# Moving maxima and logit transposes to VectorE, rounding copies to GpSimd, and the first side loads to a later unit, in a planned attention and mixture-of-experts layer

## The chip, the cores and the metric

The kernel runs on one core of a Trainium2 chip. The metric is device time in microseconds of that core; three runs of the kernel before gave a median of 3115.78 us (3114.96 to 3122.53). A difference of about 0.3% is what measurement can tell from none.

## The reference

One transformer layer in float32 over x of 4 batches, 2048 tokens, 256 channels. First attention with 16 heads of 16 channels, then a feed-forward part with a shared expert and 8 routed experts (top 2 of 8, chosen within 2 of 4 groups):

```python
x = x + attn(layernorm(x))        # 16 heads of 16; softmax(q k / 16) v; w_o, b_o, and its own + x
xf = layernorm(x).reshape(-1, 256)
scores = softmax(xf @ w_gate.T)   # 8 experts; biased, grouped top 2
shared = silu(xf @ sw1.T) * (xf @ sw3.T) @ sw2.T
out = shared.at[flat_idx].add(routed_out)   # the routed rows are added by the number in flat_idx
x = x + out
```

`flat_idx` holds expert numbers 0 to 7, so the routed results of all tokens end in the first 8 rows.

## The kernel before, in words

**Units.** Attention is cut into 64 units: one batch, one group of four heads, one chunk of 512 queries. A unit walks over 16 key tiles of 128 keys. Three kinds of TensorE (PE) work belong to it:

- `mx` (64 matmuls): scores with queries on the partitions, one PSUM bank each; VectorE (DVE) reduces each 128x512 bank to a row maximum `ms`. They run some 22 key tiles ahead of the rest.
- `st` (64 matmuls): scores with keys on the partitions, in which row 63 of the stacked queries `qst` carries the negative maximum; ScalarE (ACT) turns each bank into `et` by an exponential.
- `av` (16 groups of four matmuls, eight in the trace): the weighted sum of values, with a column of ones for the denominator.

`mx` and `st` use half of the PE's rows each (63 or 64 of 128), so two of them, one in each half, run side by side. Seven PSUM banks serve all matmuls but `av`, and a bank is reused when its reader (DVE or ACT) is done.

**From the maxima to the queries.** When a unit's last `ms` is there, `finish_mx` reduces it to `mm` (128x16) on DVE, queues a PE transpose of it to `mt` (the queue `urgent`), ACT copies it with sign changed to `mr` (16x128), and two DMAs of 4 KB write it into rows 63 and 127 of `qst`. Until then no `st` of that unit may be issued (`turned`).

**Side work.** Between the attention matmuls stand pieces of the other work, as generators that yield what they need next: `qkv_first` (load a chunk of x of a later batch, write the pad rows of its stacked keys and queries in DRAM, `kd` and `qd`), `norm`, `qkv` (transposes to channels `pt_x`, projections `pp` and `pv`), `post` (output projection `po`, second norm, transposes, shared expert `pa`, `pb`, `pd`), `route` (logits `lgT`, then their transpose `lg`), `setup` (loads and splits the weights of `post`).

**High and low parts.** float32 products are made of three matmuls on rounded numbers (fp32r): a high part h is the rounded value, a low part l the rest. In `to_channels`, `qk_proj`, `halves` and `shared` ACT writes h, in the first two straight from the PSUM bank (`S.copy(h, pt)`, or `hi` from `pp`) beside the full value (`f`, two buffers named `qkf`), and GpSimd (POOL) makes l from f and h. POOL cannot read PSUM.

**What sets the order.** A planner at build time (`Plan`, `Ahead`) gives PE, DVE and POOL a fixed order: it searches orders of `mx`, `st`, `av` and side pieces with costs written in the code. A piece tells what it costs ACT: 940 ns by default. ACT's order is fixed too, as issued. The DMA queue of SyncE (SP) is in order, and at most eight of its DMAs are under way: each waits for the one eight places before it.

**At the start.** Before unit 0 a hand-written prologue makes queries and keys of batch 0. Then `rest` makes the projections of head groups 2 and 3, the chunk loads of batch 1 start as soon as their gate is open, and `setup` is queued when unit 1 begins (`enter`). `load_unit` loads the `qst` (512 KB) of a later unit and, when the head group changes, 2 MB of keys `kst`.

All engine instructions stand under line L55 in the profile, that of a recording helper, so that one goes by tile names. A name such as `mt<-cs,mm` means tile `mt` written from `cs` (constants) and `mm`.

Of the kernel before, what the change touches and what calls it, by code (L numbers as in the profile page):

```python
# [20 lines left out]
P = 128  # L21
# [15 lines left out]
LATE = 0.01, 0.1, 16  # L37
TURNS = 1600
NET = 6
BANKS = 7  # L40
# [330 lines left out]
def const_array(rows):  # L371

    cols, at, parts = {}, 0, []

    def put(name, a):
        nonlocal at
        a = np.broadcast_to(np.asarray(a, np.float32), (P, np.shape(a)[-1]))
        cols[name] = (at, at + a.shape[1])
        parts.append(a)
        at += a.shape[1]  # L380

    i = np.arange(P)
    put("ident", np.eye(P))
    put("ones", np.ones((P, P)))
    e = np.arange(E)
    put("tri8", (e[None, :] < e[:, None]).astype(np.float32).reshape(1, -1))
    g = np.arange(4)
    put("tri4", (g[None, :] < g[:, None]).astype(np.float32).reshape(1, -1))
    put("below", (i[:, None] < np.arange(E + 1)[None, :]).astype(np.float32))
    put("pair", (i[:, None] % 64 == np.arange(64)[None, :]).astype(np.float32))  # L390
    put("eight", (i[:, None] % 32 == np.arange(8)[None, :]).astype(np.float32))
    nt = rows // P
    put("rows", (2 * (np.arange(nt)[None, :, None] * P + i[:, None, None]) + np.arange(2)[None, None, :]).reshape(P, -1))
    return np.ascontiguousarray(np.concatenate(parts, 1)), cols
# [9 lines left out]
def body(tc, B, L, cols, x, wqkv, bqk, wst, bst, bv, wo, bo, wg, w1, w2, w3, sw1, sw2, sw3, ebias, cst, pad, out):  # L404
# [20 lines left out]

    def need(kind, ns=0, *tiles, more=0):


        return kind, ns, tiles, more

    def gate(open_):

        return "g", open_, (), 0

# [122 lines left out]
    def to_channels(src, name, keep=None, fast=False, out=None):  # L557

        h, l = out or hl(f"t_{name}")
        if not fast:  # L560
            for c in range(2):
                f = keep[:, c, :] if keep is not None else sb.tile([P, QC], F32, tag="qkf", name=f"f_{name}{c}", bufs=2)
                pt = stile(f"pt_{name}{c}")
                for i in range(TQ):
                    T.transpose(pt[:, i * P:(i + 1) * P], src[:, i, c * P:(c + 1) * P], ident)
                S.copy(f, pt)
                S.copy(h[:, c, :], pt)
                G.tensor_tensor(l[:, c, :], f, h[:, c, :].bitcast(F32), ALU.subtract)
                if c == 0:
                    yield need("s1", 436)  # L570
            return h, l
        for c in range(2):
            pt = mtile(f"pt_{name}{c}")
            for i in range(TQ):
                T.transpose(pt[:, i * P:(i + 1) * P], src[:, i, c * P:(c + 1) * P], ident)
            S.copy(keep[:, c, :], pt)
            S.copy(h[:, c, :], pt)
            V.tensor_tensor(l[:, c, :], pt, h[:, c, :].bitcast(F32), ALU.subtract)
            yield
        return h, l  # L580
# [8 lines left out]
    def qk_proj(b, c, m, alloc=None):  # L589
# [15 lines left out]
        S.activation(f, pp, AF.Identity, bias=b_qk[:, m:m + 1])  # L605
        if alloc:
            S.copy(hi, f)
        else:
            S.activation(hi, pp, AF.Identity, bias=b_qk[:, m:m + 1])
        mark["G"] = G.tensor_tensor(lo, f, hi.bitcast(F32), ALU.subtract).ins  # L610
# [49 lines left out]
    def qkv_first(b, c):  # L660

        yield gate(lambda: prev(b, c, 2) in stored)
        load_x(b * NPER + c)
        tok = slice(c * QC, (c + 1) * QC)
        fill_rows(kd[b], 0, 0, H, tok)
        fill_rows(qd[b], 16, 0, H, tok)
        yield gate(lambda: prev(b, c) in stored and prev(b, c) in turned_x)
        yield need("d", 420, xin[b * NPER + c], more=3)
        yield from norm(b, c)
        normed.add((b, c))  # L670
        sums.append(store(b, c))
# [6 lines left out]
    def qkv(b, c):  # L678

        yield gate(lambda: (b, c) in normed)  # L680
        yield need("s1", 436, xls[b, c], more=1)
        xTs[b, c] = yield from to_channels(xls[b, c], f"x{b}_{c}", out=hl(f"t_x{b}_{c}", "hq"))
        turned_x.add((b, c))
        for k, m in enumerate((2, 3, 0, 1)):
            yield need("s2", 705, *xTs[b, c], more=5 - k)
            yield from qk_proj(b, c, m)
        for half in range(2):
            yield need("s2", 705, *xTs[b, c], more=1 - half)
            yield from v_proj(b, c, half)
        del xTs[b, c]  # L690
# [6 lines left out]
    def route(ch, x2T):  # L697
        n = f"{ch}"
        r = lambda nm, shape, dt=F32: sb.tile(shape, dt, tag="r_" + nm, name=f"{nm}_{n}", bufs=1)
        yield need("s1", 300, x2T)  # L700
        lgT = stile(f"lgT_{n}")
# [4 lines left out]
        f4_dead.add(f"x2T_{RN[ch]}")  # L706
        lgs = r("lgs", [P, P])
        S.copy(lgs, lgT[:, 0:P])
        yield need("m1", 109, lgs)
        lg = mtile(f"lg_{n}")  # L710
        T.transpose(lg[:, 0:P], lgs, ident)
        l3 = lg[:, 0:P].rearrange("p (t e) -> p t e", e=32)[:, :, 0:E]
        b3 = lambda a, w=E: a.unsqueeze(2).broadcast_to([P, TQ, w])
# [241 lines left out]
    def halves(b, c, ahl):  # L955

        yield gate(lambda: (b, c) in scaled)
        aT, parts = scaled.pop((b, c))
        yield need("a", 1060, aT)
        for t, np_ in parts:  # L960
            S.copy(ahl[0][0:np_, t, :], aT[0:np_, t, :])
            G.tensor_tensor(ahl[1][0:np_, t, :], aT[0:np_, t, :], ahl[0][0:np_, t, :].bitcast(F32), ALU.subtract)
        f4_dead.add(f"aT_{b}_{c}")

    def post_a(b, c, ahl=None, space=None):
# [22 lines left out]
        yield gate(lambda: f4_free(1))  # L988
        yield need("s1", 436, x2, more=1)
        x2T = f4(f"x2T_{n}")  # L990
# [37 lines left out]
    def shared(ch, n, x1, x2T, x2hl):  # L1028
# [5 lines left out]
        for m in range(2):  # L1034
# [14 lines left out]
            if m == 0:  # L1049
                yield need("s2", 705, more=1)  # L1050
        yield need("a", 920, hT)
        hhl = hl(f"hT_{n}")
        S.copy(r2(hhl[0]), r2(hT))
        G.tensor_tensor(r2(hhl[1]), r2(hT), r2(hhl[0]).bitcast(F32), ALU.subtract)
# [136 lines left out]

    urgent = deque()
    turned = set()
    qz = []

# [21 lines left out]
    def finish_mx(u, ms):  # L1217
        mm = sb.tile([P, 4 * TQ], F32, tag="mm", name=f"mm_{u}", bufs=2)
        V.tensor_reduce(mm, ms.rearrange("p h q k -> p (h q) k"), AX.X, ALU.max)

        def tr(alloc=stile):
            pt = alloc(f"mt_{u}")
            ins = T.transpose(pt[0:4 * TQ, 0:P], mm, ident).ins
            mr = sb.tile([4 * TQ, P], F32R, tag="mr", name=f"mr_{u}", bufs=2)
            S.activation(mr, pt[0:4 * TQ, 0:P], AF.Copy, scale=-1.0)
            for j in range(2):
                r0 = 64 * j + 63
                Q.dma_start(
                    qst[u % 3][r0:r0 + 1].bitcast(F32).rearrange("o p (a n) -> o (p a) n", n=P),
                    mr[2 * TQ * j:2 * TQ * j + 2 * TQ, :].bitcast(F32))  # L1230
            turned.add(u)
            return ins

        urgent.append((need("s1", 109, mm), tr))

# [120 lines left out]
    with tc.manual_schedule(engines={ENG.PE, ENG.DVE, ENG.Pool}):  # L1356
# [42 lines left out]
        load_v(0)  # L1399
        urgent.popleft()[1](mtile)  # L1400
        p30, p32 = qp(3, 0), qp(3, 2)
# [12 lines left out]
    def rest():  # L1414
        for c, m in [(c, m) for m in (1, 3) for c in range(4)]:
            yield need("s2", 705, *xTs[0, c], more=3 - c)
            yield from qk_proj(0, c, m)
        for c in range(4):
            del xTs[0, c]
# [33 lines left out]
    def enter(u):  # L1453

        b, g, c = units[u]
        if u == 1:
            posts.append(setup())
# [65 lines left out]
    def heads():  # L1523

        for n, fn in list(urgent)[:1]:
            yield n, (lambda fn=fn: (urgent.popleft(), fn()))
        for jobs in (side, sums, norms, firsts) + ((queue, posts) if due() > 0.5 * rate() else (posts, queue)):
# [3 lines left out]
    def light():  # L1531

        t, soon = plan.clock["PE"], INF
        for n, go in heads():
            kind, cost, tiles, _ = n
            if kind == "g":
# [35 lines left out]

    def urgent_now():
        while urgent:
            urgent.popleft()[1]()

    def give(c):
# [4 lines left out]
        elif c == "S":  # L1582
            u = ns // (4 * NK)
            while u not in turned:
                if nm < (u + 1) * NK * MXS:
                    do_m()
                else:
                    urgent_now()
            do_s()
# [12 lines left out]
    def present():  # L1602
# [10 lines left out]
        for n, go in heads():  # L1613
            if n[0][0] in "ms":
                ns_ = n[1] + (705 if n[0][1] == "2" else 0)
                blocks += (1 + n[3]) * [(plan.when(*n[2]) + 55, ns_, 598 if n[0][0] == "m" else 0, 160 if ns_ < 200 else 940)]
            elif n[0] == "d":
# [80 lines left out]
    with tc.manual_schedule(engines={ENG.PE, ENG.DVE, ENG.Pool}):  # L1698
        while na < NS:
# [24 lines left out]
            if plan.clock["PE"] == before:  # L1724

                urgent_now()
                plan.clock["PE"] += 500
        while urgent:
            urgent.popleft()[1]()
    ordered.__exit__(None, None, None)  # L1730
# [68 lines left out]
```

## Time and profile before

| | us |
|---|---|
| median of three runs | 3115.78 |
| the profiled execution | 3116.26 |
| its span, first to last instruction | 3114.5 |
| first exponential of unit 0 begins at about | 98 |
| PE busy, share of the span | 3022.1, 97% |
| DVE busy | 2806.9, 90% |
| ACT busy | 2510.0, 81% |
| POOL busy | 549.0, 18% |
| mean granted PE clock | 0.984 |

The page and the views are of one execution. Busy time of the PE is that of matmuls under way, with modelled ends, so a PE that is 97% busy need not be at its peak. A row of a group names engine, operation, tiles, shape and count, then busy time and mean duration, then the idle time of that engine just before and what ended it. "PEld" are weight loads, which belong to the PE's queue but overlap its matmuls.

### The profile page before, as it was taken

What the parts mean: (1) busy time and instruction counts of PE and PEld (TensorE: products, weight loads), DVE (VectorE), ACT (ScalarE), POOL (GpSimd) and SP (SyncE); (2) the same over time, 40 slices, a digit from 0 to 9 for tenths busy, and PEclk for the clock granted to TensorE, in tenths of its full rate; (3) what the DMA queues carried; (4) which work ended last, traced back from release to release, by engine and by line L of the source; (5) the groups of instructions that cost most, each with busy time, mean ns of one, the idle gap of its engine ahead of it and who ended that gap; (6) DMA issues with size and microseconds to landing.
All of it is one profiled execution on the core that took longest, in us unless ns stands there. A gap on an engine that the chain in (4) does not pass through costs nothing.

```text
span 3114.5 us, 52652 instructions
## 1 busy us (share of the span) xinstructions
PE 3022.1 (97%) x19507; PEld 1372.0 (44%) x19507; DVE 2806.9 (90%) x5049; ACT 2510.0 (81%) x4982; POOL 549.0 (18%) x503
## 2 busy tenths in 40 slices
PE   7799999999999999999999999999999999999987
PEld 5334444444444444444444444444444444444436
DVE  7689999998999999999999999899999999999926
ACT  5488888887888888888888888878887887887774
POOL 5222112211211021102211111110121111012213
PEclk9899999999999999999999999999999999999998
DMA  5644544232121212022121211212120201011200
GB/s 153 213 149 114 153 124 131 74 106 99 62 78 46 86 32 91 25 81 94 63 71 56 75 40 50 98 38 92 43 75 28 78 25 67 30 53 39 76 25 15
DMA packets 142236, 237.32 MB, mean 76 GB/s; under 512 B 13531, under 2 KB 71003, under 8 KB 137819
## 3 DMA queue, kind: packets, MB, share of 16 engines
q1 hardware_dynamic: 141979, 233.96, 23.7%
q8 instruction: 153, 2.51, 0.3%
q14 instruction: 104, 0.85, 0.1%
HBM read 138.38 MB, written 111.80 MB: 80 GB/s over the span
## 4 chain that ended last, share of the span: by engine, by line
PE 79%; DVE 14%; DMA 3%; ACT 2%; issue 1%; POOL 1%; SPq 0%; ACTq 0%; POOLq 0%; DVEq 0%
PE av L55 28%; PE mx L55 19%; PE st L55 19%; DVE ms L55 11%; PE pp L55 3%; PE po L55 2%; PE pd L55 1%; PE pv L55 1%; PE pb L55 1%; DMA qd<-hi 1%; ACT et L55 1%; PE pa L55 1%; PE pt_x L55 1%; PE mu L55 1%; PE pg L55 1%
## 5 line engine op out<-in xcount | busy, mean ns | idle before, releaser
L55 DVE TENSOR_REDUCE ms<-mx 128x1 f32<-128x512 f32 x4096 | 2533.1, 681 | 200.9 <-PE mx L55 134.2
L55 ACT ACTIVATE et<-st 128x512 f32<-128x512 f32 x4096 | 2138.1, 614 | 395.4 <-PE st L55 282.7
L55 PE MATMUL mx<-kst,qst 63*128 63x512 f32 x3984 | 1227.5, 444 | 22.9 <-DMA qst<-qd 9.9
L55 PE MATMUL st<-qst,kst 64*128 64x512 f32 x4032 | 1217.2, 443 | 25.5 <-ACT et L55 7.3
L55 PE MATMUL av<-et,vst 128*32 128x512 f32 x8192 | 1100.3, 608 | 0.0
L55 PEld LDWEIGHTS st<-qst,kst 64*128 64x128 f32 x4032 | 570.6, 186 | 604.3 <-DVE ms L55 282.4
L55 PEld LDWEIGHTS mx<-kst,qst 63*128 63x128 f32 x3984 | 575.5, 186 | 575.2 <-DVE ms L55 256.1
L55 PEld LDWEIGHTS av<-et,vst 128*32 128x32 f32 x8192 | 164.5, 108 | 326.6 <-issue 305.6
L55 POOL TENSOR_TENSOR lo<-qkf,hi 128x512 fp32r<-128x512 f32 x64 | 82.1, 1283 | 377.0 <-ACT hi L55 330.6
L55 POOL TENSOR_TENSOR th<-th,cs 128x512 f32<-128x512 f32 x32 | 33.4, 1044 | 374.6 <-ACT th L55 374.6
L55 POOL TENSOR_TENSOR aT<-aT,rb 128x512 f32<-128x512 f32 (+1 forms) x32 | 40.8, 1281 | 297.5 <-DMA rb<-rd 297.2
L55 POOL TENSOR_TENSOR hT<-hT,th 128x512 f32<-128x512 f32 x32 | 41.1, 1283 | 230.5 <-ACT hT L55 107.7
L55 ACT ACTIVATE qkf<-pp,b_qk 128x512 f32<-128x512 f32 x64 | 44.1, 689 | 45.3 <-PE pp L55 45.1
L55 POOL TENSOR_TENSOR rs_b<-rs_b,nhalf 128x4 f32<-128x4 f32 x16 | 16.3, 1017 | 230.9 <-DVE rs_b L55 185.7
L55 POOL TENSOR_TENSOR x<-x,xl 128x256 f32<-128x256 f32 x64 | 46.4, 754 | 10.6 <-ACT xl L55 10.4
L55 POOL TENSOR_TENSOR x<-x,b_o 128x256 f32<-128x256 f32 x64 | 45.3, 742 | 0.0
L55 ACT ACTIVATE hi<-pp,b_qk 128x512 fp32r<-128x512 f32 x56 | 38.3, 683 | 4.5 <-DMA qd<-hi 4.5
L55 ACT COPY ao<-av 128x512 f32<-128x512 f32 x63 | 37.9, 601 | 4.1 <-PE av L55 3.6
L55 ACT ACTIVATE xl<-x,rs_a 128x256 f32<-128x256 f32 x64 | 33.4, 595 | 9.3 <-DVE rs_a L55 9.3
L55 ACT ACTIVATE x<-x,rs_b 128x256 f32<-128x256 f32 x64 | 33.4, 597 | 7.7 <-DVE rs_b L55 7.7
L55 POOL TENSOR_TENSOR th<-th,sg 128x512 f32<-128x512 f32 x30 | 38.7, 1291 | 2.4
L55 ACT ACTIVATE hT<-pb 128x512 f32<-128x512 f32 x32 | 19.2, 600 | 22.7 <-PE pb L55 15.0
(400 smaller groups left out, 2200.1 us busy)
## 6 DMA issues: line engine op xcount, KB each, us to landing
kst<-kd SPq DMA_DIRECT2D x16, 2048.0 KB
qst<-qd SPq DMA_DIRECT2D x63, 512.0 KB
qd<-hi SPq DMA_DIRECT2D x64, 256.0 KB
kd<-hi SPq DMA_DIRECT2D x64, 256.0 KB
ad<-ao SPq DMA_DIRECT2D x63, 256.0 KB
vst<-vd SPq DMA_DIRECT2D x19, 664.0 KB
vd<-vt SPq DMA_DIRECT2D x32, 332.0 KB
x<-x SPq DMA_DIRECT2D x16, 512.0 KB
```

The costliest lines, as they stand in the source:

```text
L55: r = f(*a, **k)
```

## The change

Five edits go together.

1. **Maxima.** `finish_mx` folds the sign into the reduction, turns the 128x32 tile `mm` on DVE in blocks of 32x32 to `mt`, and four DMAs with pieces of 128 bytes write it to `qst`. The PE transpose, ACT's copy and the queue `urgent` go.
2. **Logits.** `route` turns the 128x128 logits on DVE, from PSUM to SBUF; ACT's copy `lgs`, the PE transpose `lg` and its bank go. The blocks put another order of tokens on the partitions, and the constant `rows` follows it.
3. **High parts.** In the slow form of `to_channels`, in `qk_proj` after the prologue, in `halves` and in `shared` POOL makes h from the full value, in place of ACT.
4. **Later side loads.** `qkv_first` waits until 1.5 units' worth of `st` is issued (`WARM`); `setup` is queued when unit 2 begins, not unit 1.
5. **The planner's costs.** A piece's ACT cost becomes 470, 530 or 660 in place of 940 where ACT has less to do, and the two rounding steps that move are costed on POOL.

```diff
+WARM = 1.5
...
-                S.copy(h[:, c, :], pt)
+                G.tensor_copy(h[:, c, :], f)
...
-        if alloc:
-            S.copy(hi, f)
-        else:
-            S.activation(hi, pp, AF.Identity, bias=b_qk[:, m:m + 1])
+        (S.copy if alloc else G.tensor_copy)(hi, f)
...
-        yield gate(lambda: prev(b, c, 2) in stored)
+        yield gate(lambda: prev(b, c, 2) in stored and ns > 4 * NK * WARM)
...
-        lgs = r("lgs", [P, P])
-        S.copy(lgs, lgT[:, 0:P])
-        yield need("m1", 109, lgs)
-        lg = mtile(f"lg_{n}")
-        T.transpose(lg[:, 0:P], lgs, ident)
-        l3 = lg[:, 0:P].rearrange("p (t e) -> p t e", e=32)[:, :, 0:E]
+        lg = r("lg", [P, P])
+        V.transpose(lg, lgT[:, 0:P])
+        yield need("d", 250, lg)
+        l3 = lg.rearrange("p (t e) -> p t e", e=32)[:, :, 0:E]
...
-            S.copy(ahl[0][0:np_, t, :], aT[0:np_, t, :])
+            G.tensor_copy(ahl[0][0:np_, t, :], aT[0:np_, t, :])
...
-        S.copy(r2(hhl[0]), r2(hT))
+        G.tensor_copy(r2(hhl[0]), r2(hT))
...
     def finish_mx(u, ms):
-        mm = sb.tile([P, 4 * TQ], F32, tag="mm", name=f"mm_{u}", bufs=2)
-        V.tensor_reduce(mm, ms.rearrange("p h q k -> p (h q) k"), AX.X, ALU.max)
-
-        def tr(alloc=stile):
-            pt = alloc(f"mt_{u}")
-            ins = T.transpose(pt[0:4 * TQ, 0:P], mm, ident).ins
-            mr = sb.tile([4 * TQ, P], F32R, tag="mr", name=f"mr_{u}", bufs=2)
-            S.activation(mr, pt[0:4 * TQ, 0:P], AF.Copy, scale=-1.0)
-            for j in range(2):
-                r0 = 64 * j + 63
-                Q.dma_start(
-                    qst[u % 3][r0:r0 + 1].bitcast(F32).rearrange("o p (a n) -> o (p a) n", n=P),
-                    mr[2 * TQ * j:2 * TQ * j + 2 * TQ, :].bitcast(F32))
-            turned.add(u)
-            return ins
-
-        urgent.append((need("s1", 109, mm), tr))
+        mm = mms[u % 2]
+        V.tensor_reduce(mm[:, 0:4 * TQ], ms.rearrange("p h q k -> p (h q) k"), AX.X, ALU.max, negate=True)
+        mt = sb.tile([P, 32], F32, tag="mt", name=f"mt_{u}", bufs=2)
+        V.transpose(mt, mm.bitcast(F32))
+        to = qst[u % 3].bitcast(F32).rearrange("(j r) p (a n) -> j r p a n", j=2, n=P)[:, 63]
+        for b in range(4):
+            Q.dma_start(to[:, :, :, 32 * b:32 * b + 32], mt[32 * b:32 * b + 4 * TQ])
+        turned.add(u)
...
-        if u == 1:
+        if u == 2:
             posts.append(setup())
```

More of the change, by code (lines that the diff above doesn't have):

```diff
@@ L392, in const_array @@
     nt = rows // P
-    put("rows", (2 * (np.arange(nt)[None, :, None] * P + i[:, None, None]) + np.arange(2)[None, None, :]).reshape(P, -1))
+    t = np.arange(nt)[None, :, None]
+    token = t // 4 * 512 + i[:, None, None] // 32 * P + t % 4 * 32 + i[:, None, None] % 32
+    put("rows", (2 * token + np.arange(2)[None, None, :]).reshape(P, -1))
     return np.ascontiguousarray(np.concatenate(parts, 1)), cols
@@ L424, in body, with need @@
     r2 = lambda a: a.rearrange("p a b -> p (a b)")
-    def need(kind, ns=0, *tiles, more=0):
-        return kind, ns, tiles, more
+    def need(kind, ns=0, *tiles, more=0, act=940):
+        return kind, ns, tiles, more, act
     def gate(open_):
-        return "g", open_, (), 0
+        return "g", open_, (), 0, 0
     def mtile(name):
@@ L566, in to_channels @@
                 S.copy(f, pt)
-                S.copy(h[:, c, :], pt)
+                G.tensor_copy(h[:, c, :], f)
                 G.tensor_tensor(l[:, c, :], f, h[:, c, :].bitcast(F32), ALU.subtract)
                 if c == 0:
-                    yield need("s1", 436)
+                    yield need("s1", 436, act=470)
             return h, l
@@ L680, in qkv @@
         yield gate(lambda: (b, c) in normed)
-        yield need("s1", 436, xls[b, c], more=1)
+        yield need("s1", 436, xls[b, c], more=1, act=470)
         xTs[b, c] = yield from to_channels(xls[b, c], f"x{b}_{c}", out=hl(f"t_x{b}_{c}", "hq"))
@@ L684, in qkv @@
         for k, m in enumerate((2, 3, 0, 1)):
-            yield need("s2", 705, *xTs[b, c], more=5 - k)
+            yield need("s2", 705, *xTs[b, c], more=5 - k, act=470 if k < 4 else 660)
             yield from qk_proj(b, c, m)
         for half in range(2):
-            yield need("s2", 705, *xTs[b, c], more=1 - half)
+            yield need("s2", 705, *xTs[b, c], more=1 - half, act=530)
             yield from v_proj(b, c, half)
@@ L699, in route @@
         r = lambda nm, shape, dt=F32: sb.tile(shape, dt, tag="r_" + nm, name=f"{nm}_{n}", bufs=1)
-        yield need("s1", 300, x2T)
+        yield need("m1", 300, x2T)
         lgT = stile(f"lgT_{n}")
@@ L958, in halves @@
         aT, parts = scaled.pop((b, c))
-        yield need("a", 1060, aT)
+        yield need("p", 5200, aT)
         for t, np_ in parts:
-            S.copy(ahl[0][0:np_, t, :], aT[0:np_, t, :])
+            G.tensor_copy(ahl[0][0:np_, t, :], aT[0:np_, t, :])
             G.tensor_tensor(ahl[1][0:np_, t, :], aT[0:np_, t, :], ahl[0][0:np_, t, :].bitcast(F32), ALU.subtract)
@@ L988, in post_a @@
         yield gate(lambda: f4_free(1))
-        yield need("s1", 436, x2, more=1)
+        yield need("s1", 436, x2, more=1, act=470)
         x2T = f4(f"x2T_{n}")
@@ L1050, in shared @@
                 yield need("s2", 705, more=1)
-        yield need("a", 920, hT)
+        yield need("p", 4600, hT)
         hhl = hl(f"hT_{n}")
-        S.copy(r2(hhl[0]), r2(hT))
+        G.tensor_copy(r2(hhl[0]), r2(hT))
         G.tensor_tensor(r2(hhl[1]), r2(hT), r2(hhl[0]).bitcast(F32), ALU.subtract)
@@ L1190, in load_v @@
             mark["D"] = Q.dma_start(vst[kset[u]], vd[b][:, g]).ins
-    urgent = deque()
     turned = set()
+    mms = [cp.tile([P, 32], F32R, tag=f"mm{i}", name=f"mm{i}") for i in range(2)]
+    for t in mms:
+        G.memset(t.bitcast(F32), 0.0)
     qz = []
@@ L1399, in body @@
         load_v(0)
-        urgent.popleft()[1](mtile)
         p30, p32 = qp(3, 0), qp(3, 2)
@@ L1415, in rest @@
         for c, m in [(c, m) for m in (1, 3) for c in range(4)]:
-            yield need("s2", 705, *xTs[0, c], more=3 - c)
+            yield need("s2", 705, *xTs[0, c], more=3 - c, act=470)
             yield from qk_proj(0, c, m)
@@ L1523, in heads @@
     def heads():
-        for n, fn in list(urgent)[:1]:
-            yield n, (lambda fn=fn: (urgent.popleft(), fn()))
         for jobs in (side, sums, norms, firsts) + ((queue, posts) if due() > 0.5 * rate() else (posts, queue)):
@@ L1534, in light @@
         for n, go in heads():
-            kind, cost, tiles, _ = n
+            kind, cost, tiles = n[:3]
             if kind == "g":
@@ L1571, in do_p @@
             heavy("c", INF)[1]()
-    def urgent_now():
-        while urgent:
-            urgent.popleft()[1]()
     def give(c):
@@ L1584, in give @@
             while u not in turned:
[L1585 to L1588, printed above, removed]
+                do_m()
             do_s()
@@ L1615, in present @@
                 ns_ = n[1] + (705 if n[0][1] == "2" else 0)
-                blocks += (1 + n[3]) * [(plan.when(*n[2]) + 55, ns_, 598 if n[0][0] == "m" else 0, 160 if ns_ < 200 else 940)]
+                blocks += (1 + n[3]) * [(plan.when(*n[2]) + 55, ns_, 598 if n[0][0] == "m" else 0, n[4])]
             elif n[0] == "d":
@@ L1724, in body @@
             if plan.clock["PE"] == before:
-                urgent_now()
                 plan.clock["PE"] += 500
-        while urgent:
-            urgent.popleft()[1]()
     ordered.__exit__(None, None, None)
```

## The prediction

> **What bounds it now.** I read the engines' busy times first, then long stretches side by side, then the waits in the long middle, then the first 200 us in order of time.
>
> ```profile
> PE 3022.1 (97%) x19507; PEld 1372.0 (44%) x19507; DVE 2806.9 (90%) x5049; ACT 2510.0 (81%) x4982; POOL 549.0 (18%) x503
> PE 79%; DVE 14%; DMA 3%; ACT 2%; issue 1%; POOL 1%; SPq 0%; ACTq 0%; POOLq 0%; DVEq 0%
> ```
>
> The chain that ended last is mostly PE. The table of stretches (time; busy PE, PEld, DVE, ACT, POOL; granted clock; DMA) says more:
>
> ```profile
> 300.00:2620.00 2320.00, 2301.70 (x15011) 1017.14 (x15007) 2174.95 (x3908) 1939.35 (x3840) 365.34 (x326) 1.00 0.23 73
> 2620.00:2738.00 118.00, 117.77 (x767) 48.54 (x765) 116.51 (x195) 100.83 (x199) 0.00 (x0) 1.00 0.08 27
> ```
>
> The second line is three units without side work, 39.3 us each: DVE is busy 98.7%, nearly all of it row maxima (192 of them, 116.1 us, 605 ns each). There DVE alone is the bound. The first line is ordinary life. The same table for tile `mx` counts 3309 maxima in it, 51.7 units of 64, so a unit takes 44.9 us; DVE works 42.1 of them and stands 2.8. So PE and DVE are both nearly full, and 2.8 us per unit is lost where they wait for each other or for a bank. Who held the bank is in the waits of 300 to 2620 us (total, times, longest):
>
> ```profile
> PEld st L55 <- DVE ms L55: 224.1, 326, 1.8
> PEld mx L55 <- DVE ms L55: 209.4, 326, 3.1
> PEld mx L55 <- ACT et L55: 163.1, 296, 0.8
> PEld st L55 <- ACT et L55: 160.8, 279, 1.5
> ```
>
> ACT ended 323.9 of these 757.4 us, 43%. Last, the start: PE and SP between 131 and 150 us, and ACT at 176.
>
> ```profile
> 131.19 0.80 SPq L55 DMA_DIRECT2D x<-x  x1
> 132.48 2.03 SPq L55 DMA_DIRECT2D kd<-pad  x1
> 134.55 1.16 SPq L55 DMA_DIRECT2D qd<-pad  x1
> 135.75 1.16 SPq L55 DMA_DIRECT2D qst<-qd  x1
> 133.23 0.67 PE L55 MATMUL st<-qst,kst 64*128 64x512 f32 x1 [3.64 <-ACT hi L55]
> 149.40 0.76 PE L55 MATMUL mx<-kst,qst 63*128 63x512 f32 x1 [9.91 <-DMA qst<-qd]
> 176.46 0.62 ACT L55 CAST s_3h<-wt 128x512 fp32r<-128x512 f32 x1 [6.85 <-DMA wt<-sw]
> ```
>
> PE stood 9.91 us for the queries of unit 2, whose load was issued behind 1.5 MB for batch 1 (chunk 512 KB, pad rows twice 512 KB). It stood 3.64 us because ACT's rounding `hi` waited 4.49 us for DMAs still reading that buffer. The third stall is `setup`: ACT waits for shared weights behind a 2 MB `kst`, and PE stands 5.99 us.
>
> **The change, part by part.** The sum is made against the profiled execution: 3116.26 us, of which 3114.5 span. The median, 3115.78, is 0.5 us below; I predict on the profiled one.
>
> *Start.* The order of the changed program has the load of unit 2's `qst` ahead of batch 1's pad rows and second chunk. So the 9.91 us goes, and with POOL rounding `hi`, so does ACT's wait and the 3.64 us. After the idle stretch the granted clock of 140 to 150 us is 0.68, of 150 to 160 us 0.81; I count 1.5 us for it. Together -15. The traffic comes back at unit 1.5 to 2.5, beside `kst` and the weights: I put +4. The shared-weight loads still stand behind a `kst` of 2 MB in the new order, so the third stall is kept. Sum -11; bounds 0 (the wait moves whole) and -21 (the third goes too).
>
> *PE work of the maxima.* 64 matmuls `mt`, mean 277 ns, 17.7 us. In the timeline one stands from 1025.39 to the next matmul at 1025.77, 0.38 us; the step ahead of it is 0.33 where neighbours in pairs step 0.23. With the pair that must start afresh I take 0.5 us per break, 32 us in all. In units where DVE is the bound nothing is won. The new order has 13 units without projection or output matmuls, where the old has 5, so I count 50 units, and half the value in them because DVE is nearly as full: 50 x 0.5 / 2 = -12.5.
>
> *PE work of the logits.* 16 transposes `lg` at 0.5 us, half: -4. The last stands in the final chain: ACT `lgs` (322 ns) and PE (328 ns) become one DVE instruction there, -1 with the waits between.
>
> *DVE gets.* 64 transposes of 128x32: nearest rows are the reductions of 128x32 at 177 to 180 ns; I take 180, 11.5 us. 16 of 128x128 out of PSUM: between `sc<-lg` (128x32, 191 ns) and a 128x256 statistic (411 ns); I take 300, 4.8 us. Together 16.3. DVE is the bound in the quiet units and nearly so elsewhere, so 0.6 counts: +10. Bounds: 0 if all fits into idle time, +33 at 411 ns each and full weight. Folding the sign into the reduction is taken at its present 220 ns.
>
> *ACT sheds* `hi` 38.3, the high parts of transposed tiles 34 (54 of 62), of `at` 18, of `hT` 16, `mr` 16.1, `lgs` 5.2: 128 us, 5% of its work. It has no span of its own to give; it gives banks back sooner. ACT holds 43% of the bank waits, so 0.43 x 2.8 = 1.2 us per unit is its share of the loss. A projection's bank is now read by one ACT instruction (687 ns) rather than two (687 and 683), and an exponential no longer stands behind the second. I take a third of the share, 0.4 us in 50 units: -20. Bounds 0 and -60.
>
> *POOL gets* 142 roundings of 128x512 and 15 of 128x1024. POOL's rows bound the first between a memset (526 ns) and a two-input subtraction (1283); a 128x256 copy took 390 and a 128x128 cast 289, so by 0.8 ns an element I take 590, and 1000 for the large: 99 us (89 to 218). POOL goes from 18% to 21% and is covered by its idle time. Its price without cover is a rival below.
>
> Here a page speaks against the edit. The Trainium skill, GPSIMD Engine Reference, § Performance versus the Vector engine, calls this engine the wrong place for elementwise work and gives 769 ns as measured for 512 elements of a tight loop. No row here has that shape; by that figure, an estimate, the roundings would be about 25 us longer in all, and still hidden. The Trainium skill, DMA: Bandwidth & Descriptors, opening table, asks for at least 512 bytes per piece for line rate. The old `mr` DMAs have pieces of 512 bytes, the new ones 128; no run here shows 128. By that the four would be slower than the two; the lead counted under DMAs below would still cover them.
>
> *DMAs.* Four issues on SP per unit in place of two. The two took 1.39 to 1.86 us at the start, so +1.4 to 1.9 us per unit on a queue that is idle most of 45 us. For unit 0 they now stand ahead of a `vst` load (1.15 us) and miss two engines, so I put 0. Behind them wait projections' stores, not PE. The maxima run some 22 key tiles ahead of `st`, so a unit's last maximum is there 6 key tiles (6/16 of 44.9, 17 us) before its first `st`; that covers the path. Without cover it is 2 us per unit.
>
> *Planner.* Total side work is equal; it only lies elsewhere. A line of unit time over PE side work through the old units is nearly straight, so 0, with +4 as bound.
>
> Sum: -11 - 12.5 - 4 - 1 + 10 - 20 = -38.5. 3116.26 - 38.5 = 3077.8, say **3078 us**.
>
> **Rivals.**
>
> *DVE is the whole bound (faster, little).* For it: 98.7% in quiet units. Then PE's and ACT's relief is worth nothing in the middle, DVE's 16 us count in full, and only the start (-15 at best with its clock) and end (-1) remain: about 3116. Against it: ordinary units leave DVE idle 6%.
>
> *POOL becomes ACT's brake (slower).* ACT writes the full value into `qkf`, two buffers, freed by POOL. Before, POOL read each once for 1283 ns; now it rounds first, and POOL is in order, so a rounding may stand behind a `hT` product (2.4 us) or a multiply waiting for `rb<-rd` (297.2 us of such waits in all). ACT blocked at `qkf` holds all exponentials behind it, and these hold banks. Against it: in the waits before ACT never names POOL for `qkf`, and POOL is idle 82%. It decides from 0.27 us per rounded tile (38.5 / 142); at 0.4 it costs 57 and the time is 3135.
>
> *The start doesn't change.* The wait for `qst` only moves to the next load, since SP carries the same bytes: the sum without -11, 3089. It lies inside my range.
>
> **Chances.** Forecast and its neighbours, the late start among them (3040 to 3106, little below): 0.77. DVE the whole bound, 3106 to 3125: 0.09. POOL's brake, above 3125: 0.14. The forecast's own range reaches from -75 (PE's breaks at full value, half of ACT's share) to -10. To leave no more than 2 in 10 out, I take 3042 to 3122. A difference of 0.3% (9.3 us, so under 3106 or over 3125) is what measurement tells from none: faster 0.77, same 0.09, slower 0.14.
>
> **What would show it.** Right: no PE stall over 5 us between 130 and 150 us; `mt` and `lg` gone from PE; ACT near 2382 and POOL near 650 us busy; DVE near 2823; bank waits of PE on ACT well under 43%; ordinary units near 44.4 us. Wrong: ACT waiting for POOL at `qkf`; rows `st <- DMA qst<-mt` above a few us; DVE transposes above 400 ns; ordinary units unchanged while DVE's idle time shrinks by its new work; or a new stall of 10 us at unit 2 or 3.

## The result and the profile after

| | before | changed |
|---|---|---|
| median, us | 3119.16 (3114.96 to 3124.8) | 3071.5 (3064.53 to 3073.11) |
| profiled execution, us | 3116.26 | 3064.53 |
| its span, us | 3114.5 | 3062.7 |
| units 1 to 5 begin, us | 168, 221, 269, 312, 358 | 152, 195, 255, 301, 347 |
| last exponential ends, us | 3019.9 | 2968.8 |
| mean granted PE clock | 0.984 | 0.986 |

The changed kernel takes 0.9842 of the time before (95% interval 0.9817 to 0.9866): 48 us less by the medians, 52 by the profiled executions. The medians are of four executions of each kernel; for the kernel before these are the three given above and a fourth.

First the busy times and the chain that ended last, from the page of the changed kernel (its helper line is L56, one further down):

```profile
PE 2982.9 (97%) x19427; PEld 1359.8 (44%) x19427; DVE 2823.3 (92%) x5129; ACT 2420.8 (79%) x4745; POOL 649.9 (21%) x662
PE 80%; DVE 15%; DMA 1%; issue 1%; ACT 1%; POOL 1%; SPq 0%; POOLq 0%; ACTq 0%; DVEq 0%
```

POOL and DVE land on the forecast figures (650 and 2823); ACT does not, it is busy 2420.8 us where 2382 were forecast. The shares of the chain are what they were, so no engine took over as the bound. Then the long middle, in the table of stretches (time; busy PE, PEld, DVE, ACT, POOL; granted clock; DMA):

```profile
300.00:2620.00 2320.00, 2307.54 (x15197) 1024.03 (x15198) 2225.58 (x4038) 1903.35 (x3720) 434.79 (x436) 1.00 0.23 74
```

DVE works 2225.6 us of the 2320, against 2175.0 before. Tile `mx` counts 3374 maxima in it, 52.7 units, so a unit takes 44.0 us against 44.9. DVE works 42.2 us of a unit, as before (42.1); it stands 1.8 instead of 2.8. The gain of the middle is that one microsecond. Who held PE's banks in the same stretch (total, times, longest):

```profile
PEld mx L56 <- DVE ms L56: 239.4, 357, 2.1
PEld st L56 <- DVE ms L56: 233.9, 352, 0.8
...
PEld mx L56 <- ACT et L56: 167.2, 276, 0.8
PEld st L56 <- ACT et L56: 145.7, 261, 0.8
```

ACT ends 312.9 of 786.2 us, 40%, where it was 43%. ACT lost 157 roundings, and its share of the waits hardly moved. The sum of PE's bank waits even rose, from 757.4 us to 786.2, while the unit became shorter. The change of 1 us per unit is not to be seen here; keep that in mind for the experiments. Last the start, in the rows by time (start, duration, engine, instruction; in brackets the idle time before it and what ended it):

```profile
99.54 0.61 POOL L56 CAST hi<-qkf 128x512 fp32r<-128x512 f32 x1 [6.94 <-DMA qd<-hi]
...
132.49 0.80 PE L56 MATMUL mx<-kst,qst 63*128 63x512 f32 x2 [4.16 <-DMA qst<-qd]
...
207.70 1.20 SPq L56 DMA_DIRECT2D kst<-kd  x1
209.91 2.28 SPq L56 DMA_DIRECT2D wt<-sw  x1
...
220.35 0.62 ACT L56 CAST s_3h<-wt 128x512 fp32r<-128x512 f32 x1 [6.94 <-DMA wt<-sw]
222.22 0.79 PE L56 MATMUL mx<-kst,qst 63*128 63x512 f32 x1 [9.09 <-ACT et L56]
```

The stall of 9.91 us at 149 has become one of 4.16 us at 132. The wait for `qd<-hi` is now POOL's, and in the start no other engine is seen waiting for POOL. But a stall of 9.09 us stands at 222: ACT's queue holds the rounding of a shared weight, whose load was issued behind 2 MB of `kst`; behind that rounding stand the exponentials, they hold the banks, and PE stands. This is the third stall of the prediction, and it grew from 5.99 to 9.09 us. At unit 4 the changed kernel is 11 us ahead, from there to the last exponential it gains 40 more (60 units at 44.5 against 45.1 us), the tail gives under 1.

### The profile page after: what moved, and what is told of

It reads as the page before. It is cut to its first block, busy times and chain, and to the rows that moved or that the text cites. A ratio compares the mean times of both kernels' runs of the same rounds, so it can differ in the third digit from the quotient of the medians.

```text
span 3062.7 us, 52745 instructions
## 1 busy us (share of the span) xinstructions
PE 2982.9 (97%) x19427; PEld 1359.8 (44%) x19427; DVE 2823.3 (92%) x5129; ACT 2420.8 (79%) x4745; POOL 649.9 (21%) x662
## 4 chain that ended last, share of the span: by engine, by line
PE 80%; DVE 15%; DMA 1%; issue 1%; ACT 1%; POOL 1%; SPq 0%; POOLq 0%; ACTq 0%; DVEq 0%
PE av L56 29%; PE mx L56 20%; PE st L56 19%; DVE ms L56 11%; PE pp L56 3%; PE pd L56 2%; PE pv L56 1%; PE po L56 1%; PE pt_x L56 1%; PE pa L56 1%; PE pb L56 1%; PE mu L56 1%; ACT et L56 1%; PE pg L56 1%; DVE eq L56 1%
## 5 line engine op out<-in xcount | busy, mean ns | idle before, releaser
L56 DVE TENSOR_REDUCE ms<-mx 128x1 f32<-128x512 f32 x4096 | 2521.6, 682 | 135.0 <-PE mx L56 100.5
L56 ACT ACTIVATE et<-st 128x512 f32<-128x512 f32 x4096 | 2139.9, 611 | 440.4 <-PE st L56 288.2
L56 PE MATMUL mx<-kst,qst 63*128 63x512 f32 x3984 | 1222.7, 442 | 27.9 <-ACT et L56 10.6
L56 PE MATMUL st<-qst,kst 64*128 64x512 f32 x4032 | 1221.9, 440 | 7.3 <-DMA qst<-mt 3.4
L56 PE MATMUL av<-et,vst 128*32 128x512 f32 x8192 | 1098.4, 607 | 0.8 <-ACT ao L56 0.6
L56 PEld LDWEIGHTS mx<-kst,qst 63*128 63x128 f32 x3984 | 577.7, 186 | 605.8 <-DVE ms L56 289.8
L56 PEld LDWEIGHTS st<-qst,kst 64*128 64x128 f32 x4032 | 580.8, 186 | 556.1 <-DVE ms L56 278.9
L56 PEld LDWEIGHTS av<-et,vst 128*32 128x32 f32 x8192 | 164.0, 108 | 328.4 <-issue 307.7
L56 POOL TENSOR_TENSOR aT<-aT,rb 128x512 f32<-128x512 f32 (+1 forms) x32 | 40.9, 1285 | 571.3 <-DMA rb<-rd 570.9
L56 POOL CAST hi<-qkf 128x512 fp32r<-128x512 f32 x56 | 34.2, 610 | 328.3 <-ACT qkf L56 314.3
L56 POOL TENSOR_TENSOR lo<-qkf,hi 128x512 fp32r<-128x512 f32 x64 | 82.1, 1283 | 22.9 <-ACT hi L56 13.2
L56 ACT ACTIVATE qkf<-pp,b_qk 128x512 f32<-128x512 f32 x64 | 44.0, 687 | 53.8 <-PE pp L56 53.6
L56 POOL TENSOR_TENSOR th<-th,cs 128x512 f32<-128x512 f32 x32 | 33.5, 1046 | 222.8 <-ACT th L56 222.8
L56 POOL TENSOR_TENSOR rs_b<-rs_b,nhalf 128x4 f32<-128x4 f32 x16 | 16.3, 1017 | 279.7 <-DVE rs_b L56 279.7
L56 POOL TENSOR_TENSOR hT<-hT,th 128x512 f32<-128x512 f32 x32 | 41.0, 1281 | 123.7 <-ACT hT L56 47.4
L56 POOL TENSOR_TENSOR x<-x,xl 128x256 f32<-128x256 f32 x64 | 46.4, 755 | 16.8 <-ACT xl L56 16.8
L56 POOL TENSOR_TENSOR x<-x,b_o 128x256 f32<-128x256 f32 x64 | 45.5, 740 | 0.0
L56 ACT ACTIVATE xl<-x,rs_a 128x256 f32<-128x256 f32 x64 | 33.4, 594 | 11.1 <-DVE rs_a L56 11.0
L56 ACT COPY ao<-av 128x512 f32<-128x512 f32 x63 | 37.9, 601 | 3.0 <-PE av L56 2.0
L56 POOL TENSOR_TENSOR th<-th,sg 128x512 f32<-128x512 f32 x30 | 38.9, 1296 | 2.4
L56 ACT ACTIVATE th<-pa 128x512 f32<-128x512 f32 x32 | 19.2, 599 | 24.5 <-PE pa L56 24.2
L56 ACT ACTIVATE x<-x,rs_b 128x256 f32<-128x256 f32 x64 | 33.2, 597 | 6.6 <-DVE rs_b L56 6.6
```

What stands on the lines that cost most here:

```text
L56: r = f(*a, **k)
```

## The experiments

My theory after the result was the prediction's own: each engine that is relieved gives time back by itself. The rival was that the relief matters only through the planner, which writes a new order for each edit, and that an order alone may be worth as much as a part. Twelve kernels were run. All ratios are to the kernel before, run beside it on the same chip (medians 3116.35 us for the first four, 3118.6 for the others), with 95% intervals.

### The parts, each alone

**The start alone** (edit 4).

```diff
+WARM = 1.5
...
-        yield gate(lambda: prev(b, c, 2) in stored)
+        yield gate(lambda: prev(b, c, 2) in stored and ns > 4 * NK * WARM)
...
-        if u == 1:
+        if u == 2:
```

> The kernel before with the later side loads alone (edit 4): batch 1's loads wait for 1.5 units, setup for unit 2. By the prediction's sum: -11 for the start, less the 3.6 us of the stall on ACT's rounding, which stays here: -7, so a ratio near 0.998. Rival, the wait for the unit-2 queries only moves to the next load: 0. Rival, the order is what matters (any new order of the planner moves the time by about 10 us either way, and the parts do not add up): anything from -10 to +10, with the middle of the run changed as much as the start. In the profile: no PE wait for qst<-qd over 5 us near 140 us, the setup stall of 6 us moved to about 210 us.

Measured: 3113.62 us, 0.9987 [0.9976, 0.9998], some 4 us. In its profiled execution (3107.2 us) the start itself gains what was forecast and more: unit 1 begins at 153 us and unit 4 at 299, 15 and 13 us earlier than before. From there to the last exponential the new order gives back 5 us.

**The maxima alone** (edit 1), with the order that the planner then makes.

```diff
+        V.tensor_reduce(mm[:, 0:4 * TQ], ms.rearrange("p h q k -> p (h q) k"), AX.X, ALU.max, negate=True)
...
+        V.transpose(mt, mm.bitcast(F32))
...
-        urgent.append((need("s1", 109, mm), tr))
```

> The kernel before with the maxima turned by DVE alone (edit 1). By the prediction's sum: -12.5 for PE, +7 for 64 DVE transposes (measured 211 ns each in the changed kernel, 13.5 us, weight 0.6: +8), so -5. If DVE is the whole bound: +13. If PE's breaks count in full: -32 + 8 = -24. DVE idle time per ordinary unit stays near 2.5 us by the first, falls to 2.8 less 0.2 without a gain by the second.

Measured: 3098.21 us, 0.9939 [0.9927, 0.9951], 19 us faster.

**The logits alone** (edit 2).

```diff
-        S.copy(lgs, lgT[:, 0:P])
...
-        T.transpose(lg[:, 0:P], lgs, ident)
...
+        V.transpose(lg, lgT[:, 0:P])
```

> The kernel before with the logits turned by DVE alone (edit 2). By the prediction's sum: -4 for PE, -1 at the end, +3 for 16 DVE transposes: -2, within what can be measured. If DVE is the whole bound: +4. Order theory: -10 to +10 although only 16 blocks are touched.

Measured: 3122.59 us, 1.0018 [1.0008, 1.0028], 6 us slower.

**The high parts alone** (edits 3 and 5).

```diff
-                S.copy(h[:, c, :], pt)
+                G.tensor_copy(h[:, c, :], f)
...
-            S.activation(hi, pp, AF.Identity, bias=b_qk[:, m:m + 1])
+        (S.copy if alloc else G.tensor_copy)(hi, f)
...
```

> The kernel before with the high parts rounded on POOL and the planner told of ACT's smaller costs (edits 3 and 5). By the prediction's sum: -20 for ACT's relief and -3.6 for the stall at 133 us: -24, a ratio near 0.992. If ACT's relief is worth nothing because DVE and PE are the bounds: -4. If POOL becomes ACT's brake: +10 or more, with ACT waiting for POOL at qkf. ACT near 2440 us busy, POOL near 650.

Measured: 3083.97 us, 0.99 [0.9886, 0.9915], 31 us faster.

The product of the four ratios is 0.9845, the whole measured 0.9842. So in these orders the parts add up, and two of them carry the gain. That does not yet say by which mechanism. In the table of stretches the maxima alone and the high parts alone stand so:

```profile
300.00:2620.00 2320.00, 2302.39 (x15069) 1022.46 (x15071) 2196.46 (x3988) 1948.47 (x3816) 356.92 (x316) 1.00 0.22 73
```

```profile
300.00:2620.00 2320.00, 2305.87 (x15182) 1020.62 (x15178) 2192.56 (x3947) 1899.78 (x3760) 441.08 (x442) 1.00 0.22 73
```

In both, the second the high parts, DVE works some 20 us longer in the same stretch than before (2174.95): 3338 and 3347 maxima against 3309, so 52.2 and 52.3 units. Each part takes DVE's idle time from 2.8 to 2.4 us per unit.

### What of the high parts counts

**Only the roundings whose source was a PSUM bank** (`to_channels` and `qk_proj`, with the planner's new ACT costs). The roundings of `halves` and `shared` stay on ACT: of the diff above, these lines are left as they were.

```diff
             S.copy(ahl[0][0:np_, t, :], aT[0:np_, t, :])
...
         S.copy(r2(hhl[0]), r2(hT))
```

> The kernel before with POOL rounding only where ACT read a PSUM bank twice (to_channels and qk_proj), with the planner's new ACT costs; ACT still rounds at and hT. Theory that banks come back sooner: most of the -31 us of all high parts, -25 or more. Rival, ACT's total work counts: this sheds some 60% of the work shed, so -18. Rival, the planner's costs: as in the next run.

Measured: 3108.19 us, 0.9966 [0.9954, 0.9979], 11 us.

**All high parts on POOL, the planner's ACT costs left at 940 ns.** Against the kernel with the high parts alone, `act` and all its smaller values go; the two rounding steps of `halves` and `shared` are still costed on POOL.

```diff
-    def need(kind, ns=0, *tiles, more=0, act=940):
+    def need(kind, ns=0, *tiles, more=0):
...
```

> The kernel before with all high parts on POOL, and the planner still told 940 ns of ACT for every piece. Theory that the relief itself counts: -25 to -31, near the run with new costs. Rival, the order that the planner finds from smaller ACT costs is the gain: -10 or less.

Measured: 3093.04 us, 0.992 [0.9908, 0.9933], 25 us.

Neither explanation that I had (banks given back sooner; truer costs) accounts for the whole: the kernel with the bank roundings and the true costs is the slowest of the three. The kernel with the old costs did fall where relief by itself was expected to put it (-25 to -31), the one with the bank roundings fell short of every figure expected of relief (-25 or more, or -18). Before such differences can be read, it must be known what an order is worth by itself.

### An order alone

The planner's search draws random numbers. A different seed gives another order of the same work.

```diff
-        self.random = Random(1).random
+        self.random = Random(2).random
```

> The kernel before with another seed of the planner's random search, nothing else: the work is the same, only its order differs. It sizes what an order is worth. If the parts measured so far are effects of the work itself, this gives 0 +- 6 us. If order is the cause of the maxima's -19 and the high parts' -31, this moves by 15 us or more.

Measured: 3136.41 us, 1.006 [1.0048, 1.0073], **18 us slower**, with no instruction added or removed.

The same with seed 3:

> The kernel before with a third seed. Two orders of it gave 3116 and 3136 us. If the shipped order is a lucky one: 3125 to 3140. If the second was an outlier: 3110 to 3122.

Measured: 3119.06 us, 0.9998 [0.9989, 1.0007], no difference.

The changed kernel with seed 2:

> The changed kernel with the seed 2 that cost the kernel before 18 us. If the gain of the change is in the work: 3085 to 3095, 45 us or so below the kernel before with the same seed. If the changed kernel's order is the luck: 3110 or more.

Measured: 3095.52 us, 0.9923 [0.991, 0.9935]; that is 41 us below the kernel before at the same seed, 0.9923 / 1.006 = 0.9864. Three orders of the old work lie between 3116 and 3136 us, two of the new between 3071 and 3096, and at both seeds tried the whole is over 40 us faster. So a lucky order does not explain the gain of the whole. But the seed is worth 24 us in the changed kernel, more than in the kernel before. The single parts are another matter: 6, 11 or 19 us is no more than a seed can be worth, and 31 us not much more.

### The same order, other engines

These two experiments ask what the moved work is worth where the order stays. The planner goes on booking the old instructions, so that it writes the old order, but the work is given to the other engine.

**The maxima, order held.** The planner books a PE transpose and an ACT copy that are not issued. The order of PE is that of before without its 64 `mt`, that of DVE is that of before with 64 transposes more, ACT has 64 copies less.

```diff
+        plan.book_dve("tensor_reduce", mm[:, 0:4 * TQ], [ms.rearrange("p h q k -> p (h q) k")], {})
+        nc.vector.tensor_reduce(mm[:, 0:4 * TQ], ms.rearrange("p h q k -> p (h q) k"), AX.X, ALU.max, negate=True)
...
+        nc.vector.transpose(mt, mm.bitcast(F32))
...
-            ins = T.transpose(pt[0:4 * TQ, 0:P], mm, ident).ins
...
-            S.activation(mr, pt[0:4 * TQ, 0:P], AF.Copy, scale=-1.0)
...
+            plan.book_pe("transpose", pt, [mm[:, 0:4 * TQ], ident], {})
+            plan.book_act("activation", Held(f"mr_{u}"), [pt], {})
```

> Edit 1 with the order held: the planner books the PE transpose and ACT's copy of the maxima as before and so puts every mx, st, av and side piece where the kernel before has it; DVE turns the maxima in truth, and PE and ACT have 64 instructions fewer. What the work itself is worth without a new order. Prediction's sum: -5 to -6. PE's breaks in full: -24. DVE the whole bound: +13. If the -19 measured with a new order was mostly the order, this is near -5 or 0.

Measured: 3128.97 us, 1.0033 [1.0021, 1.0045]: **10 us slower**, where the same edit with a new order was 19 us faster.

**The high parts, order held.** ACT has 157 roundings less, POOL 157 more; the orders of PE and DVE are those of before, instruction by instruction.

```diff
-                S.copy(h[:, c, :], pt)
+                plan.book_act("copy", h[:, c, :], (pt,), {})
+                nc.gpsimd.tensor_copy(h[:, c, :], f)
...
-            S.activation(hi, pp, AF.Identity, bias=b_qk[:, m:m + 1])
+            plan.book_act("activation", hi, (pp, b_qk[:, m:m + 1]), {})
+            nc.gpsimd.tensor_copy(hi, f)
...
```

> Edit 3 with the order held: the planner books ACT's rounding as before, so that PE, DVE and the rest of ACT keep their order word for word; POOL rounds the 157 tiles in truth. Prediction's sum: -20 and -3.6 for the stall at 133 us, -24. Rival, ACT's relief is worth nothing in itself and only lets the planner find a better order: 0 to -4. The rounding on POOL with a new order gave -25 (old costs) and -31 (new costs).

Measured: 3120.69 us, 1.0009 [1.0, 1.0018]: **nothing**, where the same edit with a new order gave 31 us. Its busy times and its stretch:

```profile
PE 3021.6 (97%) x19507; PEld 1368.9 (44%) x19507; DVE 2811.8 (90%) x5049; ACT 2430.5 (78%) x4825; POOL 649.5 (21%) x660
```

```profile
300.00:2620.00 2320.00, 2298.61 (x14984) 1013.47 (x14980) 2175.86 (x3902) 1873.99 (x3709) 444.08 (x448) 0.99 0.23 73
```

The work did move: ACT is down by 80 us and POOL up by 100. But DVE works 2175.9 us of the stretch, as before (2175.0), on 51.6 units (before 51.7). The waits agree:

```profile
PEld st L55 <- DVE ms L55: 231.1, 337, 2.3
PEld mx L55 <- DVE ms L55: 211.3, 334, 3.0
PEld mx L55 <- ACT et L55: 163.0, 281, 1.6
PEld st L55 <- ACT et L55: 158.5, 265, 0.8
```

ACT still ends 321.5 us of PE's bank waits; before they were 323.9. These waits name the exponentials. Taking 157 roundings from between them did not bring the exponentials that PE waits for forward by anything that counts. With the orders of PE and DVE fixed, a gap stays where the order put it. At the start the 3.6 us that were forecast are not won either: PE comes earlier to the queries of unit 2 and waits for their load 17.68 us, where it was 9.91.

```profile
148.93 0.76 PE L55 MATMUL mx<-kst,qst 63*128 63x512 f32 x1 [17.68 <-DMA qst<-qd]
```

The same table for the maxima with the order held:

```profile
300.00:2620.00 2320.00, 2292.47 (x14897) 1010.11 (x14893) 2174.47 (x3943) 1927.05 (x3771) 361.85 (x321) 0.99 0.23 73
```

3294 maxima, 51.5 units. DVE has the transposes to do in the same working time, and PE's freed slots win nothing: its busy time falls by 9 us (from 2301.70) and its idle time grows by as much. A unit takes 45.1 us against 44.9, longer by about the 0.21 us of one transpose. That points to DVE, near the +13 us expected if DVE is the whole bound; the granted clock has a share in it too (last section), and the two were not separated.

### The new stall at the start

The changed kernel with the splitting of each half of the shared weights half a unit after its load, so that ACT does not reach the rounding before the weights are there.

```diff
             t = load_w(src, "sth", 2)
+            due_ = ns + 32
+            yield gate(lambda: ns >= due_)
             yield need("a", 530, t)
```

> The changed kernel, with each of the four shared weights split half a unit after its load is issued rather than as soon as the planner thinks it landed. ACT then no longer waits 6.9 us for wt<-sw behind the 2 MB of kst, with PE idle 9 us near 215. Theory that this is a stall at the head of ACT's queue: -9 to -11 against the changed kernel, so about 3061. Rival, the wait only moves to another load: 0.

Measured: 3061.45 us (3058.92 to 3065.42), 0.9819 [0.9805, 0.9832], the lowest median of all. Units 3 to 5 begin at 245, 291 and 337 us, 9 to 11 before those of the changed kernel, and PE's wait of 9.09 us is gone. So ACT's wait for the weights was its cause. That the whole is faster by as much is not settled: the changed kernel's interval (0.9817 to 0.9866) overlaps, and the two profiled spans are 3063.0 and 3062.7 us, since the new order gives 8 us back in the middle (3362 maxima against 3374).

## Why the prediction was right in sum, and wrong in its terms

The forecast was 3078 us, and the time is 3071.5. The agreement is largely luck, because the terms reached the sum by another way than the prediction told. By its terms, as written down before the runs, the start, the maxima, the logits and the high parts were to give -7, -5, -2 and -24 us; each alone measured -4, -19, +6 and -31. Only the sums, -38 and -48, are near each other.

**The planner's zero** is the step that failed. The prediction said: "Total side work is equal; it only lies elsewhere [...] so 0, with +4 as bound." The gain appeared only with a new order: the high parts gave 31 us with a new order and nothing with the old one, the maxima gave 19 us with a new order and cost 10 with the old one. I had treated the order as a condition and the engines' relief as the cause. In this kernel PE, DVE and POOL run a list that was written beforehand; in these two experiments freed time became shorter units only when the list put other work there.

**ACT's relief, -20**, was a third of ACT's share of the bank waits. With the order held it is 0 (+2 us), and the sign that the prediction named for it, bank waits on ACT "well under 43%", came out at 40%. With a new order it is -31. The step behind the term was to share out DVE's 2.8 us of idle time per unit by PE's bank waits, which are 14.7 us per unit; nothing in the record ties the one to the other. The relief itself was over-rated: the 128 us are durations added up, but ACT's busy time fell by 89, because its instructions overlap. In the kernel before, the 4096 exponentials of 614 ns add up to 2515 us and keep ACT busy 2138.1:

```profile
L55 ACT ACTIVATE et<-st 128x512 f32<-128x512 f32 x4096 | 2138.1, 614 | 395.4 <-PE st L55 282.7
```

**PE's maxima, -12.5**, with a right count (64 `mt` gone) and a wrong effect: with the order held the edit is not negative at all, with a new order it is -19; both include DVE's part.

**The logits, -4 and -1**, measured +6 alone, within what an order is worth. The end kept its part: the tail went from 94.6 to 93.8 us.

**The start, -11**, is -11 by unit 4 in the whole change and -13 by unit 4 with the edit alone, but over its whole run that edit gave only 4. That the stall at 149 goes was right. That the third stall is "kept" was too mild: it grew to 9.09 us, in the manner the prediction listed under "Wrong" (a new stall of 10 us at unit 2 or 3).

**DVE's +10.** The durations were under-rated by little, as the groups of the changed kernel show (engine, operation, tiles, shape, count; busy time, mean ns; idle time before):

```profile
L56 DVE STREAM_TRANSPOSE mt<-mm 128x32 f32<-128x32 f32 x64 | 13.5, 212 | 2.2
L56 DVE STREAM_TRANSPOSE lg<-lgT 128x128 f32<-128x128 f32 x16 | 4.9, 306 | 2.9 <-PE lgT L56 2.9
...
L56 POOL CAST hi<-qkf 128x512 fp32r<-128x512 f32 x56 | 34.2, 610 | 328.3 <-ACT qkf L56 314.3
```

212 ns stand for the 180 taken and 306 for 300, 18.4 us in all where 16.3 were counted. POOL's 610 ns stand for 590, and its idle time before `hi` is a wait for ACT's `qkf`, never the reverse: in the waits ACT names only PE for `qkf`. So POOL's brake, the rival on the slower side, did not come. The rounding of 128x512 by itself runs nearer to 590 than to the 769 ns that the Trainium skill, GPSIMD Engine Reference, § Performance versus the Vector engine, gives for 512 elements; here the measurement decides, for a one-input cast. Whether it would hold in a loop of POOL alone, no run here shows.

**The DMAs, 0**, held: the four issues have a median of 506 ns each, and PE's `st` waits for `qst<-mt` 3.4 us in the whole run.

**DVE as the whole bound, near 3116**, did not come either. DVE's work per unit stayed at 42 us, its idle time fell by a third.

**What stays open.** The seeds show that the whole gain outlives one change of order. For the single parts they do not: whether the 19 us of the maxima and the 31 of the high parts are what the planner can make of such relief, or partly chance, was tried with one order each; the 11 us of the bank roundings beside the 31 of all may be the same chance. The opposite trial, the new order with the old division of work, was not run; that the gain needs the relief too is argued from two other seeds of the old work, neither of which was faster. The 10 us that the maxima lose with the order held are not divided between DVE's added work and the clock either: see the last section.

## What to carry to other kernels

Where engines run an order that was planned ahead, try an edit twice, once with the old order held and once with a new one: the first tells what the relief is worth in that order (here nothing), the second what the planner makes of it. Before parts are read, find what an order alone is worth by changing the seed of the search; here that was 18 us in one kernel and 24 in the other, as much as most of the parts under study. And an instruction that waits for a load, placed in an in-order queue ahead of instructions that free banks, hands its wait to TensorE: here 6.94 us at ACT's weight rounding were 9.09 us at PE.

## What the runs showed of the hardware

The granted clock of PE fell to half for some microseconds in the midst of busy stretches, at times after a short idle moment. In the maxima with the order held, by short stretches (columns as above, the granted clock third from the end):

```profile
1110.00:1112.00 2.00, 1.48 (x5) 0.89 (x5) 2.00 (x4) 2.00 (x5) 2.00 (x4) 1.00 0.01 2
1112.00:1114.00 2.00, 2.00 (x11) 0.63 (x12) 1.86 (x4) 1.17 (x3) 2.00 (x4) 0.67 0.09 18
1114.00:1116.00 2.00, 2.00 (x10) 0.80 (x8) 1.64 (x3) 1.32 (x3) 0.41 (x1) 0.50 0.32 109
1116.00:1118.00 2.00, 2.00 (x10) 0.38 (x10) 2.00 (x4) 1.06 (x2) 0.00 (x0) 0.50 0.72 216
1118.00:1120.00 2.00, 2.00 (x14) 0.98 (x14) 0.29 (x2) 0.69 (x2) 0.00 (x0) 0.62 0.75 235
```

PE stood about half a microsecond at 1110 us; from 1112.7 the granted clock is 0.5 for 6.8 us, with PE busy throughout. The kernel before has a longer gap of 1.45 us at 1847 without it:

```profile
1846.00:1850.00 4.00, 2.55 (x21) 1.09 (x18) 3.93 (x8) 1.97 (x5) 1.23 (x1) 1.00 0.44 134
```

And half a clock came without any gap: in the maxima with the order held PE is busy without a break between 1490 and 1498 us, and from 1498.4 the granted clock is 0.5 for 6.8 us.

```profile
1490.00:1498.00 8.00, 8.00 (x45) 3.27 (x41) 7.76 (x23) 7.91 (x17) 1.33 (x2) 1.00 0.41 149
1500.00:1502.00 2.00, 2.00 (x11) 0.50 (x3) 2.00 (x6) 0.03 (x1) 0.00 (x0) 0.50 0.03 8
```

So a gap does not decide it, and what does, these runs do not show. The Trainium skill, TensorE: Matmul & The Clock Gate, § Why this matters for your kernels, asks for no idle gaps over some 3 us; here gaps of a fifth of that stood before half a clock, while others of half that length passed. In the stretch from 300 to 2620 us the time lost to these moments, each duration by the missing part of the clock, is 5.1 us before, 13.7 in the maxima and 11.9 in the high parts with the order held, 17.1 with seed 2, and 1.7 in the changed kernel. These are single executions, and that of the kernel before was one with a higher clock than most.

What this costs can be estimated from the 54 executions of the kernel before that stand beside the experiments. Program and order are the same in all of them, and the mean granted clock lies between 0.981 and 0.986: the eight at 0.981 have a median of 3121.6 us, the three at 0.986 one of 3114.6, so 7 us go with 0.005. With the order held the executions of the maxima have 0.9815 in the mean and those of the high parts 0.9823, those of the kernel before beside them 0.9830. By that, an estimate, the clock stands for some 2 of the 10 us that the maxima lose and for 1 of the 2 of the high parts; with seed 2 (0.9810 against 0.9826) for 2 of the 18. The clock was not tried by itself.
